# Preparing the last layer's first half batch in a lane of layer 2

## The chip, the cores and the metric

The kernel is one program for one core of a Trainium2 chip. The metric is device time of one execution in microseconds (us), lower is better; the figure quoted is the median of several runs. Everything is computed in fp32. Five engines run their own instruction streams in order and wait for each other through semaphores: TensorE (PE, matrix products), VectorE (DVE), ScalarE (ACT), GpSimd (POOL, which here issues the gathers and scatters) and SyncE (SP, which issues the other transfers).

## The reference

Four layers work on a residual `x` of 4 sequences, 1024 tokens each, 128 channels. Each layer adds half a feed-forward block, a whole "attention" block, and half the same feed-forward block again:

```python
x = x + 0.5 * L0_ffn(ln(x)); x = x + L0_attn(ln(x)); x = x + 0.5 * L0_ffn(ln(x))
x = x + 0.5 * L1_ffn(ln(x)); x = x + L1_attn(ln(x)); x = x + 0.5 * L1_ffn(ln(x))
x = x + 0.5 * L2_ffn(ln(x)); x = x + L2_attn(ln(x)); x = x + 0.5 * L2_ffn(ln(x))
x = x + 0.5 * L3_ffn(ln(x)); x = x + L3_attn(ln(x)); x = x + 0.5 * L3_ffn(ln(x))
```

`L2_ffn` is a mixture of 8 experts, of which each token uses the best 2 (128 -> 512 -> 128, relu). `L2_attn` is a linear attention with one decay `gamma`. Layer 3, cut to what matters:

```python
def L3_attn(x):                       # 16 heads of 8 channels, y_t depends on all t' < t
    xx = shift(x) - x                 # the token before, minus this one
    m = tanh((x + xx * maa_x) @ w1)   # five small mixes, one for each of w k v r g
    xw, xk, xv, xr, xg = (x + xx * (maa_i + m_i @ w2_i) for i in "wkvrg")
    r, k, v, g = xr @ W_r, xk @ W_k, xv @ W_v, silu(xg @ W_g)
    wdec = exp(-exp(time_decay + tanh(xw @ dw1) @ dw2))
    for t in range(T):                # the recurrence, for each head
        kv = outer(k[t], v[t]); y[t] = r[t] @ (S + u * kv); S = S * wdec[t] + kv
    return (groupnorm(y) * gamma + beta) * g @ W_o

def L3_ffn(x):                        # xr, xk mix a token with the one before
    return sigmoid(xr @ W_r.T) * (square(relu(xk @ W_k.T)) @ W_v.T)
```

## The kernel before, in words

The residual stays on the chip as four tiles `X[b]` (128 channels x 1024 tokens, `x0` to `x3`). `run` goes through the stages l0, l1_attn, l2 and l3; layer 1's feed-forward blocks are run inside l0 and l2.

**Lanes.** Within a stage, work is written as tasks: generators that record some instructions and then yield an estimated cost. `lanes` takes several lists of tasks. A task starts when the tasks that it names are done and the one ahead of it in its lane is finished; of the tasks that are running, the one with the lowest clock goes on. That settles the order in which the program is recorded. The framework below it then settles the order of each engine's stream, and adds the waits, also those for memory: a tile that is laid over the place of older tiles waits until these have been used for the last time. Pools are stacked from the left or the right end of the on-chip memory, and a pool that is opened later takes the place of one that was closed.

**Layer 2** (`layer2`, `macaron`). The tokens are routed and run through the experts in two groups, A = sequences 0 and 1, and Z = 2 and 3, and that twice (`n` = 0 ahead of the attention, 1 behind it). The lanes of the stage are: the four expert runs; the combines, which fetch the results of a sequence and add them to its `X`; two lanes with layer 1's last feed-forward blocks (`first0` to `first3`) and the attention of the four sequences (`middle0` to `middle3`); and the routes. `experts` works in blocks of 128 slots, 39 for a group: SP loads the block's expert weights (`e_w`, five buffers), POOL gathers 128 token rows (`e_xg`, L452), PE turns them (L456), multiplies up in four products and down in four (L229), ACT applies the bias and the relu between (`e_h`, L466), DVE adds the last bias (`e_y`, L477) and POOL scatters (`res`, L478). `combine` loads `c_y` from `res`, weighs (L508, L509), turns (L512) and adds. The last run of experts, n = 1 with group Z, starts when everything else of layer 2 but combine 10, 11 (sequences 0, 1) and combine 12, 13 is over.

`l2_decay` makes the decay matrix `G` and its row `grow` (L853 to L865) for the attention, in a pool of its own (`l2d`) at the right end. Nothing else needs them before `middle0`. They depend only on weights.

**Layer 3** (`layer3`). Eight units: four sequences, two halves of 512 tokens. Each unit has a front (`l3_ffn`, then `l3_prepare`, which makes `wdec`, `k`, `vals`, `r`, `g` and the first part of `y`), the recurrence (`l3_recur`), and an end (`l3_finish`, and `l3_ffn` again). There are five lanes: one of recurrences in the order 00, 10, 01, 11, 20, 30, 21, 31 (sequence, half), two of ends and two of fronts (even and odd sequences). The fronts of even sequences keep their tiles in `l3even` and those of odd ones in `l3odd`, at the right end. `normed` is the layer norm at the head of each part: centre (a product with `x`), square (`n_sq`), four small products, the root on ACT (`n_std`, L956), the reciprocal on DVE (`n_r`, L957), four products that spread it, and `xn` (L966). A whole stage ends before the next one starts to be recorded, so all eight fronts are recorded behind layer 2.

Of the kernel before, what the change touches and what calls it, by code (L numbers as in the profile page):

```python
# [18 lines left out]
B, S, D = 4, 1024, 128  # L19
# [188 lines left out]
class Macaron:  # L208
# [959 lines left out]
        v.tensor_tensor(X, X, o, ALU.add)  # L1168
        yield 6

    def layer3(self, f, t, c3):
        sb = lambda name, bufs=2, **k: self.tc.tile_pool(name=name, bufs=bufs, reuse_waits="tile", **k)
        with ExitStack() as ctx:
            enter = ctx.enter_context
            wave, accs, tail, prep = (
                enter(self.psum(name, n)) for name, n in (("l3wave", 2), ("l3acc", 1), ("l3tail", 2), ("l3prep", 3))
            )

            tmp, *front = (enter(sb(name, side="right")) for name in ("l3tmp", "l3even", "l3odd"))
            rec, *end = (enter(sb(name)) for name in ("l3rec", "l3ends0", "l3ends1"))  # L1180
            given, carries, seen = {}, {}, {}
            start = lambda f, *a: lambda: f(*a)
            units = [(b + i, h) for b in range(0, B, 2) for h in range(2) for i in range(2)]
            fronts, recs, ends = ([], []), [], ([], [])
            for b, h in units:
                u = f"{b}{h}"
                mine = given[b, h] = {}
                wp, wend = front[b % 2], end[b % 2]
                s = [seen.setdefault((b, i), {}) for i in range(3)]
                fronts[b % 2].extend([  # L1190
                    (f"ffn{u}0", (), start(self.l3_ffn, prep, tmp, wp, f, b, h, s[0])),
                    (f"prepare{u}", (), start(self.l3_prepare, prep, tmp, wp, t, c3, b, h, s[1], mine)),
                ])
                recs.append((f"recur{u}", (f"prepare{u}",), start(self.l3_recur, wave, accs, rec, c3, b, h, carries, mine)))
                ends[b % 2].extend([
                    (f"finish{u}", (f"recur{u}",), start(self.l3_finish, tail, wend, t, c3, b, h, mine)),
                    (f"ffn{u}1", (), start(self.l3_ffn, tail, tmp, wend, f, b, h, s[2])),
                ])
            self.lanes(recs, *ends, *fronts)
# [71 lines left out]
    def layer2(self, moe, m, right, enter, ffn):  # L1271
        A, Z = (0, 1), (2, 3)
        side, main = self.side, self.main
        decay = self.l2_decay(side, enter(right, "l2d"), m, self.c2)
        early = right.enter_context(ExitStack())
        pf = [enter(early, f"l1f1{i}") for i in range(2)]
        pa = []

        def swap():

            early.close()
            pa.extend(enter(right, f"l2a{i}") for i in range(2))
            yield 0

        def more(route):
# [12 lines left out]
        self.macaron("l2", moe, AF.Relu, ([A, Z], [A, Z]), marks, more)  # L1298

    def run(self, stages):  # L1300
        nc = self.nc
        self.X = []
# [14 lines left out]
        tags = {"l1a": "attn_w", "l3a": "attn_w", "c1": "attn_c", "c2": "attn_c", "c3": "attn_c"}  # L1317
        have = {}

        def weights(name):  # L1320
            if name not in have:
                have[name] = self.l1_weights() if name == "l1f" else self.load(name, tag=tags.get(name))
            return have[name]

        sb = lambda name, bufs=2, **k: self.tc.tile_pool(name=name, bufs=bufs, reuse_waits="tile", **k)
        for n, name in enumerate(stages):
            for s in stages[n : n + 2]:
                for w in needs[s]:
                    weights(w)
            if name in ("l0", "l2"):  # L1330
                with self.psum("main", 4) as self.main, self.psum("side", 4) as self.side, sb(name + "moe") as self.fp:
                    moe = dict(weights(name + "s"))
                    moe["both"] = self.t(self.res, [P, P + NE], "both", bufs=2)
                    nc.vector.tensor_copy(moe["both"][:, 0:P], self.c0["center"])
                    nc.scalar.copy(moe["both"][:, P:], self.centered(moe["rw"], NE))
                    with ExitStack() as right:
                        enter = lambda stack, name, bufs=2: stack.enter_context(sb(name, bufs, side="right"))
                        m = dict(weights(name + "a"))
                        ffn = lambda wp, ps, b: lambda: self.l1_ffn(ps, wp, weights("l1f"), b)
                        if name == "l2":  # L1340
                            self.c2 = weights("c2")
                        if name == "l0":
                            self.layer0(moe, m, right, enter, ffn)
                        else:
                            self.layer2(moe, m, right, enter, ffn)
            elif name == "l1_attn":
                with sb("ln1") as self.lnp:
                    self.l1_attn(weights("l1a"), weights("c1"))
            else:
                f, t, c3 = self.l3_ffn_weights(weights("l3f")), self.l3_time_weights(weights("l3a")), weights("c3")  # L1350
                self.layer3(f, t, c3)
        for b in range(B):
            nc.sync.dma_start(out=self.out[:, b * S : (b + 1) * S], in_=self.X[b])

# [35 lines left out]
```

## Time and profile before

| | us |
|---|---|
| median of 3 runs (3131.44 to 3135.03) | 3132.94 |
| the profiled execution, whole | 3239.76 |
| its span in the profile | 3237.5 |
| layer 1's attention ends (its last add to `x3`, L807) | 2030.6 |
| combine 11 ends, from here the last experts are alone | 2623.5 |
| last product of the last experts | 2722.0 |
| first product of layer 3 | 2742.6 |
| end of the span | 3237.5 |

The profile is of one execution, and it was longer than the runs without it. Its rows show, for a group of instructions, the engine, the operation, what it writes and reads, the shape, how many there were, how long they took, and the idle time ahead of them with what ended it. `x0`, `n_r` and the like are the program's tile names; L229 is the line of a helper through which nearly all products are recorded, so products are told apart by tile and shape. An fp32 product stands in the trace as two matmul records. PEclk is the clock that TensorE was granted in a stretch, 1.00 being full speed.

### The profile page before, as it was taken

To read this page: it belongs to the slowest core of one execution; us is meant where nothing else is said; L and a number is where in the kernel's file an instruction comes from. 1 tells how busy PE (TensorE), PEld (TensorE's weight loads), DVE (VectorE), ACT (ScalarE), POOL (GpSimd) and SP (SyncE) were. 2 spreads that over 40 slices of the span, in tenths; PEclk is the share of its full clock that TensorE was granted. 3 is DMA by queue.
4 is the path that set the end of the run, shared out by engine and by line. 5 is a ranking of instruction groups with operands and counts; after the bars stand their busy time and mean duration, and the time that the engine had idled before them with its cause. 6 is when DMAs were issued, how large, how long until landed. Compare 5 with 4: busy or idle time off the path is not lost. (4 is left out here: it accounts for less than half of the span.)

```text
span 3237.5 us, 47507 instructions
## 1 busy us (share of the span) xinstructions
PE 2766.3 (85%) x17694; PEld 1584.7 (49%) x17694; DVE 1834.3 (57%) x3214; ACT 1626.5 (50%) x3631; POOL 799.3 (25%) x748
## 2 busy tenths in 40 slices
PE   5877537778969999999999999987988976899997
PEld 4666415665633333333333333567877865334333
DVE  3476986774226676676677673452565622354764
ACT  3555524657712565566465666444453544345342
POOL 3566306552440000000000000046434463010110
PEclk8889758889977999999999999989998988788997
DMA  6656415563500000000000000057665675000000
GB/s 211 208 169 196 125 50 160 159 188 119 154 19 9 5 6 4 6 5 6 20 6 4 3 1 1 21 166 233 198 186 163 209 228 162 0 1 1 7 7 13
DMA packets 122886, 277.57 MB, mean 86 GB/s; under 512 B 18016, under 2 KB 67296, under 8 KB 122528
## 3 DMA queue, kind: packets, MB, share of 16 engines
q1 hardware_dynamic: 101792, 231.77, 23.7%
q0 software_dynamic: 20864, 42.77, 4.5%
q8 instruction: 140, 2.29, 0.3%
q14 instruction: 90, 0.74, 0.1%
HBM read 238.43 MB, written 31.85 MB: 83 GB/s over the span
## 5 line engine op out<-in xcount | busy, mean ns | idle before, releaser
L736 DVE TENSOR_REDUCE nm<-two 128x2 f32<-128x1024 f32 x512 | 626.6, 1224 | 290.8 <-PE s L229 271.4
L759 ACT ACTIVATE e<-s 128x512 f32<-128x512 f32 x1024 | 555.8, 595 | 408.7 <-PE s L229 405.7
L466 ACT ACTIVATE e_h<-bank,e_w 128x128 f32<-128x128 f32 x1304 | 451.0, 367 | 495.3 <-PE bank L229 382.9
L229 PE MATMUL bank<-e_x,e_w 128*128 128x128 f32 x2608 | 543.6, 312 | 127.9 <-ACT e_h L466 65.7
L229 PE MATMUL s<-qm,kz 32*128 32x512 f32 x2048 | 635.7, 645 | 0.8 <-ACT e L759 0.8
L229 PE MATMUL two<-kz,qz 32*128 32x512 f32 x2048 | 595.0, 666 | 21.4 <-POOL va L724 2.5
L452 POOL DMA_INDIRECT e_xg<-rows,g_source x326 | 331.6, 1017 | 822.1 <-DVE g_target L419 356.1
L229 PE MATMUL bank<-e_w,e_h 128*128 128x128 f32 x2608 | 475.5, 298 | 56.7 <-ACT e_h L466 31.3
L229 PEld LDWEIGHTS bank<-e_x,e_w 128*128 128x128 f32 x2608 | 413.4, 205 | 219.9 <-ACT e_h L466 113.1
L478 POOL DMA_INDIRECT res<-e_y,g_target x326 | 368.6, 1131 | 300.1 <-DVE e_y L477 135.4
L229 PEld LDWEIGHTS bank<-e_w,e_h 128*128 128x128 f32 x2608 | 387.6, 206 | 89.8 <-ACT e_h L466 46.6
L229 PE MATMUL o<-e,va 128*32 128x256 f32 x4096 | 329.2, 393 | 0.1
L229 PEld LDWEIGHTS two<-kz,qz 32*128 32x128 f32 x2048 | 160.1, 189 | 240.5 <-issue 163.3
L229 PEld LDWEIGHTS o<-e,va 128*32 128x32 f32 x4096 | 81.0, 108 | 391.8 <-issue 371.8
L458 DVE COPY e_x<-bank 128x128 f32<-128x128 f32 x326 | 92.7, 285 | 263.7 <-PE bank L456 139.7
L477 DVE TENSOR_TENSOR e_y<-bank,e_w 128x128 f32<-128x128 f32 x326 | 93.6, 287 | 213.9 <-PE bank L229 191.0
L229 PEld LDWEIGHTS s<-qm,kz 32*128 32x128 f32 x2048 | 207.0, 184 | 10.9 <-issue 7.8
L724 POOL COPY va<-vd 128x256 f32<-128x256 f32 x16 | 6.7, 431 | 626.2 <-PE o L229 537.9
L1131 POOL TENSOR_TENSOR z<-st,r 128x512 f32<-128x512 f32 x32 | 46.2, 1444 | 417.5 <-DVE st L1124 240.2
L456 PE MATMUL bank<-c,e_xg 128*128 128x128 f32 x326 | 97.0, 300 | 39.7 <-DMA e_xg<-rows,g_source 36.2
L466 ACT ACT_TABLE_LOAD x53 | 68.0, 1283 | 24.0 <-PE bank L229 18.0
L544 DVE TENSOR_TENSOR prod<-qkv 128x2048 f32<-128x2048 f32 x32 | 73.1, 2286 | 5.5 <-ACT qkv L536 5.5
(304 smaller groups left out, 3489.0 us busy)
## 6 DMA issues: line engine op xcount, KB each, us to landing
e_w<-in_l0m_dram SPq DMA_DIRECT2D x170, 578.0 KB
e_w<-in_l2m_dram SPq DMA_DIRECT2D x156, 578.0 KB
c_y<-res SPq DMA_DIRECT2D x32, 512.0 KB
rows<-g_xt SPq DMA_DIRECT2D x16, 512.0 KB
e_xg<-rows,g_source POOLq DMA_INDIRECT x326
res<-e_y,g_target POOLq DMA_INDIRECT x326
x<-in_x_dram SPq DMA_DIRECT2D x4, 512.0 KB
qz<-qd SPq DMA_DIRECT2D x64, 32.0 KB
```

The lines of the kernel that those rows point to most:

```text
L229: self.nc.tensor.matmul(out, lhsT, rhs, start=start, stop=stop)
L452: nc.gpsimd.indirect_dma_start(out=xg, out_offset=None, in_=rows[:, :], in_offset=at(source[:, k : k + 1]))
L456: nc.tensor.transpose(tp, xg, self.c0["ident"])
L458: nc.vector.tensor_copy(x, tp)
L466: nc.scalar.activation(h[:, fc, :], o[:, fc, :], func, bias=w[:, 2 * FC * P + fc : 2 * FC * P + fc + 1])
L477: nc.vector.tensor_tensor(y, o, w[:, MOE_W - D :], ALU.add)
L478: ins = nc.gpsimd.indirect_dma_start(out=res[:, :], out_offset=at(target[:, k : k + 1]), in_=y, in_offset=None)
L544: v.tensor_tensor(pr, q.unsqueeze(2).to_broadcast(sh), k.unsqueeze(1).to_broadcast(sh), ALU.mult)
L724: nc.gpsimd.tensor_copy(va[n % RING][:, :, :, 1 : 1 + HD], dense[b, "vd"][:, :, 32 * g4 : 32 * g4 + 32].rearrange("p t (h d) -> p t h d", ...
L736: v.tensor_reduce(nm[:, it, h, 2 * pair : 2 * pair + 2], s, AX.X, ALU.max, negate=True)
L759: nc.scalar.activation(es[g], s, AF.Exp, scale=scale)
L1131: (pool if i else v).tensor_tensor(z, st[:, 0:HALF], r, ALU.mult)
```

## The change

The front of layer 3's first unit (sequence 0, first half) becomes a lane of layer 2. A task `clear` waits until all four attentions of layer 2 are over, closes their pools, opens layer 3's pools `l3tmp` and `l3even` in their place, makes layer 3's scaled weights, and adds two tasks to its own lane: `ffn000`, which waits for combine 10, and `prepare00`. They use the `side` PSUM pool of layer 2. `layer3` then leaves this front out, and its first recurrence waits for nothing. So that the attention's pools can be closed ahead of layer 2's end, the pool `l2d` of the decay goes to the left end, where it lies in the place of layer 1's attention.

```diff
+    def l3_front(self, b, h, prep, wp, after=()):
+        l3, u = self.l3, f"{b}{h}"
+        f, t, c3 = l3["weights"]
+        mine = l3["given"].setdefault((b, h), {})
+        s = [l3["seen"].setdefault((b, i), {}) for i in range(2)]
+        return [
+            (f"ffn{u}0", after, lambda: self.l3_ffn(prep, l3["tmp"], wp, f, b, h, s[0])),
+            (f"prepare{u}", (), lambda: self.l3_prepare(prep, l3["tmp"], wp, t, c3, b, h, s[1], mine)),
+        ]
+
+    def l3_open(self):
+        sb = lambda name: self.l3_pools.enter_context(self.tc.tile_pool(name=name, bufs=2, reuse_waits="tile", side="right"))
+        w = self.weights
+        self.l3.update(
+            weights=(self.l3_ffn_weights(w("l3f")), self.l3_time_weights(w("l3a")), w("c3")),
+            given={}, seen={}, tmp=sb("l3tmp"), even=sb("l3even"), begun=[],
+        )
...
-            tmp, *front = (enter(sb(name, side="right")) for name in ("l3tmp", "l3even", "l3odd"))
+            tmp, given, seen = (l3[k] for k in ("tmp", "given", "seen"))
+            front = l3["even"], enter(sb("l3odd", side="right"))
...
-                fronts[b % 2].extend([
-                    (f"ffn{u}0", (), start(self.l3_ffn, prep, tmp, wp, f, b, h, s[0])),
-                    (f"prepare{u}", (), start(self.l3_prepare, prep, tmp, wp, t, c3, b, h, s[1], mine)),
-                ])
-                recs.append((f"recur{u}", (f"prepare{u}",), start(self.l3_recur, wave, accs, rec, c3, b, h, carries, mine)))
+                begun = (b, h) in l3["begun"]
+                if not begun:
+                    fronts[b % 2].extend(self.l3_front(b, h, prep, front[b % 2]))
+                mine = given[b, h]
+                s = {2: seen.setdefault((b, 2), {})}
+                after = () if begun else (f"prepare{u}",)
+                recs.append((f"recur{u}", after, start(self.l3_recur, wave, accs, rec, c3, b, h, carries, mine)))
...
     def lanes(self, *lanes):
-        lanes = [list(lane) for lane in lanes]
...
-        decay = self.l2_decay(side, enter(right, "l2d"), m, self.c2)
+        decay = self.l2_decay(side, enter(right, "l2d", side="left"), m, self.c2)
+        late = right.enter_context(ExitStack())
...
-            pa.extend(enter(right, f"l2a{i}") for i in range(2))
+            pa.extend(enter(late, f"l2a{i}") for i in range(2))
             yield 0
+
+        def clear():
+            late.close()
+            self.l3_open()
+            self.l3["begun"].append((0, 0))
+            lane.extend(self.l3_front(0, 0, side, self.l3["even"], ("combine10",)))
+            yield 0
+
+        lane = [("clear", [f"middle{b}" for b in range(B)], clear)] if self.goes_on else []
...
                     route(1, A, "middle0", "middle1", "combine01"), route(1, Z, "middle2", "middle3", "combine03"),
                 ],
+                lane,
```

The order of the instructions on each engine, as the two programs have it: the front's products stand between those of about 12.5 expert blocks, beginning at the end of combine 11, and 24 blocks follow them. Layer 3's first recurrence stands right behind combine 13 on DVE. The 23 instructions of `l2_decay` that stood in two places among layer 1's attention on DVE stand behind the last add to `x3` (L807), ahead of layer 2's first `xc` (L614), and PE multiplies `G` ahead of the first product with `x0`. On SP the load of layer 3's constants `c3`, which takes the place of the decay's, goes behind the load of `l3a`; the other orders of SP and POOL differ only by exchanges of neighbours.

More of the change, by code (lines that the diff above doesn't have):

```diff
@@ L1169, in l3_finish, with layer3 @@
         yield 6
-    def layer3(self, f, t, c3):
+    def l3_front(self, b, h, prep, wp, after=()):
[14 more added lines that the diff above has]
+        )
+    def layer3(self):
+        if not self.l3:
+            self.l3_open()
+        l3 = self.l3
+        f, t, c3 = l3["weights"]
         sb = lambda name, bufs=2, **k: self.tc.tile_pool(name=name, bufs=bufs, reuse_waits="tile", **k)
@@ L1177, in layer3 @@
             )
-            tmp, *front = (enter(sb(name, side="right")) for name in ("l3tmp", "l3even", "l3odd"))
+            tmp, given, seen = (l3[k] for k in ("tmp", "given", "seen"))
+            front = l3["even"], enter(sb("l3odd", side="right"))
             rec, *end = (enter(sb(name)) for name in ("l3rec", "l3ends0", "l3ends1"))
-            given, carries, seen = {}, {}, {}
+            carries = {}
             start = lambda f, *a: lambda: f(*a)
@@ L1186, in layer3 @@
                 u = f"{b}{h}"
-                mine = given[b, h] = {}
-                wp, wend = front[b % 2], end[b % 2]
-                s = [seen.setdefault((b, i), {}) for i in range(3)]
-                fronts[b % 2].extend([
-                    (f"ffn{u}0", (), start(self.l3_ffn, prep, tmp, wp, f, b, h, s[0])),
-                    (f"prepare{u}", (), start(self.l3_prepare, prep, tmp, wp, t, c3, b, h, s[1], mine)),
-                ])
-                recs.append((f"recur{u}", (f"prepare{u}",), start(self.l3_recur, wave, accs, rec, c3, b, h, carries, mine)))
+                wend = end[b % 2]
+                begun = (b, h) in l3["begun"]
[5 more added lines that the diff above has]
+                recs.append((f"recur{u}", after, start(self.l3_recur, wave, accs, rec, c3, b, h, carries, mine)))
                 ends[b % 2].extend([
@@ L1281, in swap @@
             early.close()
-            pa.extend(enter(right, f"l2a{i}") for i in range(2))
+            pa.extend(enter(late, f"l2a{i}") for i in range(2))
             yield 0
+        def clear():
+            late.close()
+            self.l3_open()
+            self.l3["begun"].append((0, 0))
+            lane.extend(self.l3_front(0, 0, side, self.l3["even"], ("combine10",)))
+            yield 0
+        lane = [("clear", [f"middle{b}" for b in range(B)], clear)] if self.goes_on else []
         def more(route):
@@ L1301, in run @@
         nc = self.nc
-        self.X = []
+        self.X, self.l3, self.l3_pools, self.goes_on = [], {}, ExitStack(), "l3" in stages
         self.c0 = self.load("c0")
@@ L1323, in weights @@
             return have[name]
+        self.weights = weights
         sb = lambda name, bufs=2, **k: self.tc.tile_pool(name=name, bufs=bufs, reuse_waits="tile", **k)
@@ L1336, in run @@
                     with ExitStack() as right:
-                        enter = lambda stack, name, bufs=2: stack.enter_context(sb(name, bufs, side="right"))
+                        enter = lambda stack, name, bufs=2, side="right": stack.enter_context(sb(name, bufs, side=side))
                         m = dict(weights(name + "a"))
@@ L1349, in run @@
             else:
-                f, t, c3 = self.l3_ffn_weights(weights("l3f")), self.l3_time_weights(weights("l3a")), weights("c3")
-                self.layer3(f, t, c3)
+                self.layer3()
+                self.l3_pools.close()
         for b in range(B):
```

## The prediction

> **What bounds the kernel now.** I read the page's slices first, then the change's three places: a table of windows, the timeline of PE, the groups of one window. The page has PE busy 85% of the span; what counts is which wait ends last in each place. Columns of the first fence: stretch, length, then busy us of PE, PE's weight loads, DVE, ACT, POOL, then PE's granted clock and the DMA.
>
> ```profile
> 2450.00:2550.00 100.00, 98.19 (x698) 88.21 (x698) 63.46 (x205) 41.50 (x110) 46.54 (x48) 0.99 0.55 169
> 2623.00:2722.00 99.00, 81.91 (x581) 70.08 (x579) 17.95 (x67) 46.08 (x136) 58.85 (x61) 1.00 0.74 226
> 2722.00:2742.00 20.00, 4.97 (x17) 3.03 (x17) 6.25 (x20) 4.89 (x16) 0.97 (x1) 0.60 0.41 112
> 2742.00:2813.00 71.00, 61.27 (x157) 27.56 (x157) 16.39 (x37) 28.04 (x44) 0.00 (x0) 0.75 0.00 0
> 2813.00:2853.00 40.00, 38.41 (x98) 17.23 (x102) 22.95 (x42) 15.98 (x30) 6.02 (x4) 0.79 0.00 1
> 2853.00:3158.00 305.00, 291.44 (x911) 121.41 (x904) 182.47 (x276) 137.21 (x246) 34.72 (x24) 0.91 0.01 4
> 3158.00:3237.00 79.00, 58.78 (x168) 26.07 (x166) 31.87 (x44) 20.93 (x38) 5.48 (x5) 0.78 0.03 14
> ```
>
> The last experts alone (2623 to 2722) leave PE 18% idle: no engine is full, and their 33.9 blocks (305 products, nine a block) take 2.92 us each. Beside the attention (2450 to 2550) PE is full. Layer 3's middle, 2853 to 3158, is PE's: 291 of 305 us. Its head is PE's too, at clock 0.75. The next fences show PE at that seam: the drain of the experts, 9.00 and 5.58 us of waiting for the last combines, then the first two fronts; and its clock.
>
> ```profile
> 2722.04 0.49 PE L229 MATMUL bank<-e_w,e_h 128*128 128x128 f32 x2 [0.23 <-ACT e_h L466]
> 2731.53 2.01 PE L512 MATMUL bank<-c,c_y 128*128 128x128 f32 x7 [9.00 <-DVE c_y L509]
> ...
> 2761.65 1.02 PE L229 MATMUL bank<-xn,now_k 128*128 128x512 f32 x2
> 2762.51 1.02 PE L229 MATMUL bank<-xn,past_k 128*128 128x512 f32 x2
> ...
> 2776.22 3.89 PE L229 MATMUL bank<-t,attn_w 128*128 128x512 f32 x4 [2.39 <-DVE t L1042]
> ```
>
> ```profile
> 2748.00:2754.00 6.00, 5.31 (x18) 0.50 0.00 0
> 2754.00:2760.00 6.00, 5.35 (x13) 0.50 0.00 0
> 2760.00:2766.00 6.00, 6.00 (x16) 1.00 0.00 0
> ```
>
> **What a front costs.** At full clock a 512-wide product starts every 0.86 us (2761.65, 2762.51). `ffn000`: 6 such (5.2), and its norm's four 1-wide and four 128-wide products (8 records in about 0.5 and 0.95): 6.6 us. `prepare000`: 16 such (13.8), two side-by-side pairs of 1.06, a norm of 1.5: 17.4. Together 24.0 us of PE at full clock. With the recurrence (6.4), the finish (4.1) and the second `ffn` (6.6) a unit is 41.1, layer 3 eight times that, 329.
>
> **Layer 3 loses a front.** Counted in the program's order, 211 us of those 329 lie between the rows at 2853 and 3158, where the first and sixth recurrences' sums end; they take 305 us, 1.445 us for each full-clock us (clock 0.91, changes of weights and shapes, short waits). 24.0 x 1.445 = 34.7 us. It is off the end's path only as far as PE stays the bound. At the head the first recurrence now runs beside the next two `ffn`: eight kv (0.68), eight scans (1.21) and four z (0.67) are 18 us of DVE, which had only 16.4 us of work in the head's 71, so it fits, but the fronts' norms queue behind the scans: I give back 2 us. **-33**, from -42 (idle PE in the head filled as well) to -22 (the head's chains stretch, and only the head's 24 us at full clock are won).
>
> **The head's clock.** The trace has PE at 0.50 from about 2725 to 2760, though it was busy 5.3 of 6 us from 2748. The Trainium skill (TensorE: Matmul & The Clock Gate, Part 1) has half clock only until about 3.4 us of sustained activity. By that rule the cold stretch ends near 2746 and only some 3 us of layer 3's first work is slow; by the trace it is 17 us. Does moving the front out of a cold stretch gain more? By the trace no: the gap of 2722 to 2742 stays, and the same cold stretch then falls on the next front. So I count full-clock us at the middle's rate. By the rule the head would cost some 7 us less before and after alike, and the sum would be the same.
>
> **The last experts gain a front.** 24.0 us of PE come among 12.5 blocks that took 36.5 us. What is free? In 2450 to 2550, PE full, 24 blocks went beside 44.5 us of attention products (same spacings, 0.11 a record and in proportion to width), so a packed block costs (100 - 44.5) / 24 = 2.3 us. Then 12.5 x 2.3 + 24.0 = 52.8, **+16.3**. To that come waits of the front's own chain, since PE takes its products in order and the blocks behind them wait:
>
> ```profile
> L229 PE MATMUL bank<-c,n_r 128*128 128x128 f32 x32 | 8.3, 440 | 3.4 <-DVE n_r L957 3.4
> L229 PE MATMUL bank<-c,n_sq 128*128 128x1 f32 x32 | 6.0, 310 | 2.7 <-ACT n_sq L950 2.7
> L229 PE MATMUL bank<-t,attn_w 128*128 128x512 f32 x4 | 3.1, 860 | 2.4 <-DVE t L1042 2.4
> ```
>
> These rows of the head (2745 to 2813), with 0.7 ahead of `x`, are 9.2 us for two fronts, 4.6 for one; the blocks between fill about half: +2.5. ACT gets eleven times about 0.6 and five table loads of 1.28, 13 to 16 us, where it is 46% busy; a relu caught behind a load makes PE wait for `e_h`: +2. Against it, while PE is held the weights of the next blocks land, and one or two blocks then run at 2.3 or 2.56 (the drain's pace) instead of 2.92 us until these are used up: -4. Sum **+17**, from +7 (idle PE takes nearly all, catch-up of two more blocks) to +30 (none is used). The loads and gathers are not more; they are only later, since SP's `e_w` waits for a buffer that the delayed `e_y` frees, and POOL's gathers for PE's turns.
>
> **The decay moves.** Layer 2's decay leaves layer 1's attention. There it did cost something:
>
> ```profile
> 1581.93 0.23 DVE L857 COPY G<-attn_c 128x128 f32<-128x128 f32 x1 [1.99 <-DMA attn_c<-in_c_dram]
> ...
> 1586.01 1.21 DVE L736 TENSOR_REDUCE nm<-two 128x2 f32<-128x1024 f32 x1
> ```
>
> The reduce at 1586.01 stood behind the series though its product began at 1582.6, and PE idled 1.94 us for it: **-2**. At the new place DVE has 8 x 0.16, 15 x about 0.26, then two copies of 0.6 and a reciprocal between: 7 us behind the last L807, so `G` is done near 2037, and the first product with `x0`, at 2026.2 before, waits on PE until then. `x0`'s norm takes 6 us more: both first products come at 2043 instead of 2037.4 and 2040.5. Six gate and up products were done by 2045.0 and will be near 2048.5: **+4**, to +8 if PE comes back cold, +1 if the order of `x1` covers it. It is not hidden: PE is full from 2045, and routes and experts wait for these. The load of `c3`, now behind the decay, has until layer 3; on SP the row writes behind it come 50 us later.
>
> **Sum.** -33 + 17 - 2 + 4 = -14 us in the profiled execution of 3239.76. The median is 3132.94, 3.3% less; I scale to -13.5 and predict **3120**. The measurement can tell about 0.2%, 6.3 us.
>
> **Rivals.**
> 1. *The blocks pay for it all (slower).* Every link of the front's chain holds PE, because few block products stand between: behind the first norm's small products there are three, 0.6 us, against a table load, a root and a reciprocal of 1.28 + 0.26 + 0.17. Then 24 us, 4.6 us of links and 6.4 us of table loads all add, with 5 us more for blocks that miss their turn: +40, and -33 + 40 + 2 = +9, 3142. It decides from +31, when the 12.5 blocks take 5.4 us each. For it: PE's order is fixed. Against: the attention's chains packed well. 0.24.
> 2. *The experts hide it (much faster).* The weights set the pace, so front and blocks only fill PE's 18%, and the loads run ahead: +7, sum -24, 3109. For it: DMA 0.74 busy at 226 GB/s, blocks of 1.9 us at 2624.66 to 2628.45. Against: five buffers, of which four are in use. 0.18.
> 3. *Layer 3 is not shortened by its products.* The recurrences are one lane, and if their turns with DVE and POOL set the middle, a missing front only leaves PE idle: layer 3 gains 12, the sum is +7, 3140. Against: PE 291 of 305. 0.12. That the front is not moved at all is excluded by the order.
>
> The likeliest, 0.46, gives 3120 with 3111 to 3130. Faster by over 0.2%: 0.39 of it, rival 2 whole: 0.57. Slower: 0.20 of rival 1, 0.05 of rival 3, 0.01 of the likeliest: 0.26. The rest, 0.17, within. Range 3104 to 3145: the lower half of rival 2 and the upper third of rival 1 are cut.
>
> **What would show it.** The profile after should have the experts from combine 11 to their last product at about 116 us instead of 99, PE over 90% busy in the front's stretch; the first recurrence's sum about 35 us behind layer 3's first product (110 before), layer 3 some 33 us shorter; PE's products with `x0` in layer 2 about 10 us after L807. Wrong if the experts grow by over 30 us (rival 1), under 10 (rival 2), or layer 3 shortens by under 20 (rival 3).

## The result, and the profile after

The changed kernel takes 3118.43 us (median of 22 runs, 3108.86 to 3130.17); before takes 3129.45 us on the same chip (22 runs, 3123.61 to 3135.53). The ratio is 0.9966, with an interval of 0.9957 to 0.9976: 10.6 us less by the ratio, 7.5 to 13.5 by the interval. The prediction was 3120, from 13.5 us less. The experiments ran on three chips on which before took 3251 to 3266 us; what that makes of the change is part of the explanation. The record does not name the chip of this first comparison. The profiled execution of the changed kernel has a span of 3118.9 us.

First the table of windows of the changed kernel: stretch, length, busy us of PE, PE's weight loads, DVE, ACT and POOL, PE's granted clock, DMA share, GB/s.

```profile
2540.00:2591.00 51.00, 49.94 (x256) 32.31 (x255) 14.39 (x36) 28.78 (x66) 19.77 (x20) 1.00 0.52 154
2591.00:2645.00 54.00, 53.71 (x416) 50.42 (x414) 14.01 (x48) 32.69 (x98) 39.48 (x41) 1.00 0.87 279
2645.00:2665.00 20.00, 6.06 (x21) 3.27 (x21) 6.28 (x20) 4.88 (x16) 1.52 (x2) 0.57 0.41 111
2665.00:2736.00 71.00, 67.64 (x193) 29.76 (x193) 33.83 (x67) 28.07 (x52) 5.65 (x4) 0.81 0.00 1
2736.00:2776.00 40.00, 39.22 (x109) 18.86 (x109) 17.68 (x32) 16.86 (x29) 3.10 (x2) 0.83 0.00 1
2776.00:3040.00 264.00, 256.15 (x770) 105.64 (x769) 153.24 (x233) 112.22 (x204) 28.95 (x20) 0.89 0.01 4
3040.00:3118.00 78.00, 59.70 (x173) 27.59 (x172) 37.28 (x51) 22.48 (x42) 8.41 (x6) 0.76 0.03 14
```

The first row is the front among the expert blocks: PE is busy 49.9 of 51 us. In the second, the 24.4 blocks behind it, PE has hardly any idle time: 2.22 us a block, at 279 GB/s, where before's profile had 2.91 us and 226 GB/s. The third row is the drain, as empty as before. In layer 3's head (fourth row) PE is busy 67.6 of 71 us, against 61.3; DVE has twice the work, since the first recurrence now runs there.

The seam in PE's timeline (start, length, engine, line, operation; in brackets the idle time and what ended it), and behind it PE's clock (stretch, length, PE busy, clock, DMA share, GB/s):

```profile
2644.94 0.49 PE L229 MATMUL bank<-e_w,e_h 128*128 128x128 f32 x2 [0.23 <-ACT e_h L466]
2645.36 1.13 PE L1026 MATMUL wave<-vals,attn_c 32*128 32x512 f32 x4
2654.34 2.05 PE L512 MATMUL bank<-c,c_y 128*128 128x128 f32 x7 [7.86 <-DVE c_y L509]
...
2662.89 2.05 PE L512 MATMUL bank<-c,c_y 128*128 128x128 f32 x7 [5.64 <-DVE c_y L509]
```

```profile
2665.00:2671.00 6.00, 5.67 (x13) 0.50 0.01 3
2671.00:2677.00 6.00, 5.22 (x10) 0.50 0.00 0
2677.00:2683.00 6.00, 6.00 (x16) 0.50 0.00 1
2683.00:2689.00 6.00, 6.00 (x23) 0.52 0.00 0
2689.00:2695.00 6.00, 6.00 (x16) 1.00 0.00 0
```

The recurrence's first products (`wave`) run at the start of the drain; the next ones come only behind it, at 2667.44. The cold stretch is not gone; it lasts some 24 us into layer 3. Of the front's own waits the groups of the front's stretch show almost nothing:

```profile
L229 PE MATMUL bank<-c,n_r 128*128 128x128 f32 x16 | 2.2, 280 | 0.6 <-DVE n_r L957 0.6
L229 PE MATMUL bank<-c,n_sq 128*128 128x1 f32 x16 | 2.1, 253 | 0.0
L229 PE MATMUL bank<-t,attn_w 128*128 128x512 f32 x2 | 1.0, 594 | 0.0
```

0.6 us, where the head of before had 8.5 us in these rows for two fronts: the blocks between fill it.

### The profile page after: what moved, and what is told of

It is laid out like the page before. It is cut to its first block, busy times and chain, and to the rows that moved or that the text cites. A ratio compares the mean times of both kernels' runs of the same rounds, so it can differ in the third digit from the quotient of the medians.

```text
span 3118.9 us, 47516 instructions
## 1 busy us (share of the span) xinstructions
PE 2740.2 (88%) x17694; PEld 1580.9 (51%) x17694; DVE 1831.6 (59%) x3214; ACT 1616.8 (52%) x3627; POOL 796.0 (26%) x748
## 4 chain that ended last, share of the span: by engine, by line
PE 67%; DVE 6%; ACT 3%; DMA 3%; POOL 2%; issue 1%; POOLq 0%; SPq 0%; ACTq 0%; DVEq 0%
PE bank L229 32%; PE two L229 18%; PE o L229 8%; PE s L229 5%; DVE nm L736 2%; PE wave L1026 2%; DMA c_y<-res 1%; DMA e_xg<-rows,g_source 1%; ACT e_h L466 1%; PE bank L1026 1%; PE bank L456 1%; PE acc L1026 1%; POOL kz L669 0%; DMA e_w<-in_l2m_dram 0%; DMA res<-e_y,g_target 0%
## 5 line engine op out<-in xcount | busy, mean ns | idle before, releaser
L736 DVE TENSOR_REDUCE nm<-two 128x2 f32<-128x1024 f32 x512 | 626.0, 1224 | 289.8 <-PE s L229 269.6
L229 PE MATMUL bank<-e_w,e_h 128*128 128x128 f32 x2608 | 465.6, 293 | 26.3 <-ACT e_h L466 17.4
L229 PEld LDWEIGHTS bank<-e_w,e_h 128*128 128x128 f32 x2608 | 381.6, 203 | 49.7 <-ACT e_h L466 30.5
L458 DVE COPY e_x<-bank 128x128 f32<-128x128 f32 x326 | 92.7, 285 | 199.4 <-PE bank L456 181.1
L1131 POOL TENSOR_TENSOR z<-st,r 128x512 f32<-128x512 f32 x32 | 46.1, 1441 | 384.8 <-DVE st L1124 318.6
L1026 PE MATMUL wave<-vals,attn_c 32*128 32x512 f32 x128 | 74.3, 761 | 3.7 <-DVE kv L1117 3.6
```

The costliest lines, as they stand in the source:

```text
L229: self.nc.tensor.matmul(out, lhsT, rhs, start=start, stop=stop)
L458: nc.vector.tensor_copy(x, tp)
L736: v.tensor_reduce(nm[:, it, h, 2 * pair : 2 * pair + 2], s, AX.X, ALU.max, negate=True)
L1026: i = self.nc.tensor.matmul(out, lhsT, rhs, start=start, stop=stop).ins
L1131: (pool if i else v).tensor_tensor(z, st[:, 0:HALF], r, ALU.mult)
```

## Where the time went, in all profiles

All profiles, cut at the same events: the first and last row of layer 1's attention (L736, L807), the last product of combine 03 and of combine 11, the last expert product, the last product of combine 13, the end. us of each piece. The kernels are those of the experiments below; rows with one number in the first column ran on one chip (a dash: not known).

| chip | kernel | to the attention | attention | to combine 03 | to combine 11 | last experts | drain | layer 3 |
|---|---|---|---|---|---|---|---|---|
| - | before (first profile) | 968.3 | 1062.3 | 414.4 | 178.5 | 99.0 | 19.8 | 495.2 |
| - | after | 924.2 | 1057.6 | 393.4 | 164.9 | 105.3 | 19.9 | 453.6 |
| 5 | ctrl (before) | 984.6 | 1062.3 | 417.8 | 182.0 | 104.2 | 20.1 | 493.2 |
| 5 | decay_left | 986.5 | 1056.8 | 433.6 | 181.5 | 104.1 | 20.1 | 492.3 |
| 5 | front_only | 984.0 | 1059.8 | 416.0 | 176.8 | 120.8 | 20.1 | 449.5 |
| 5 | late76 | 987.5 | 1056.6 | 434.1 | 180.6 | 113.9 | 26.0 | 455.0 |
| 8 | ctrl2 (before) | 978.2 | 1062.6 | 414.0 | 177.6 | 102.7 | 19.8 | 495.9 |
| 8 | after2 | 989.8 | 1057.7 | 422.1 | 179.4 | 121.3 | 19.8 | 440.9 |
| 8 | late76_right | 979.5 | 1059.7 | 415.4 | 177.8 | 109.1 | 25.7 | 445.3 |
| 8 | front_plus | 972.8 | 1059.8 | 411.6 | 177.3 | 121.6 | 19.4 | 472.9 |
| 1 | ctrl3 (before) | 981.7 | 1060.5 | 421.7 | 182.0 | 105.3 | 19.8 | 495.7 |
| 1 | warm_before | 978.5 | 1062.3 | 418.9 | 177.9 | 107.1 | 19.3 | 493.9 |
| 1 | warm_front | 977.6 | 1062.3 | 418.6 | 177.1 | 121.3 | 19.6 | 450.2 |
| 1 | ffn_only | 972.0 | 1061.4 | 421.5 | 182.3 | 107.9 | 19.9 | 457.4 |

Two things are read from it. All four profiles of before are of one kind, with spans of 3237.5 to 3266.8 us, also the one that the prediction had; none is of an execution of 3130. And after and after2 are the same kernel, 112 us apart: the attention is equal to 0.1 us, and after2 is longer in every stretch with experts (the first, the third, the fourth and the fifth column, 125 us together); its layer 3 was 13 us shorter. Executions like that of after are called short below, and those like after2 and the four of before long.

It is easy to take the weights for the cause, since the long executions move fewer GB/s, but the traces speak against it. In after2, for the blocks behind the front (2700 to 2770), these are all the waits of PE, and the largest of SP's, which issues the weights (us in total, times, the longest):

```profile
PE bank L229 <- ACT e_h L466: 8.0, 9, 2.0
PE bank L229 <- issue: 1.6, 5, 0.6
PE bank L229 <- DVE e_x L458: 0.4, 1, 0.4
```

```profile
SPq L450 <- DVE e_y L477: 21.2, 10, 4.2
```

PE waits for no load; the loads wait for buffers that the blocks free. Followed one by one from issue to last packet to first product, the weights of after2 were in place 1.4 us or more ahead of their use (4.5 in the median), those of before 2.6 or more, those of ctrl2 3.7 or more. In after, the short execution, it was 1.7 us in the median, and once nothing. So late weights are not the cause, and the low rate goes with the slow blocks without making them slow. What does differ is when the results of PE arrive: DVE copies a turned block (`e_x`, L458) at most 0.14 us behind the end of PE's record in after, up to 1.6 us behind it in after2 and 1.9 in before. What holds them back no run shows, so the cause of the long executions stays open.

## The experiments

Ratios are against before on the same chip, with their 95% intervals.

**Before once more** (`ctrl`, no edit).

> The kernel before, profiled once more. The first profile of before was about 107 us longer than its median, and had its last experts at 2.92 us a block; after has them at 2.16 us a block behind the front, PE full. Theory (that execution's transfers were slow): here the span is near 3127, the stretch from combine 11's end to the last expert product is about 77 us (2.25 us a block, PE over 93% busy), the tail 20 us, layer 3 about 494 us. Rival (the front itself lets the weights run ahead): the stretch is again near 99 us, 2.9 us a block, and the 107 us are elsewhere.

It took 3266.4 us, its last experts 104.2 us. The theory needed a 3130 us execution to show itself, and this was none, so the two were not told apart by the time. Slow transfers as its reason do not fit the trace: here too the weights landed 2.7 us or more ahead of their first product. ctrl2 and ctrl3 below repeat the run, with the same outcome.

**The decay alone** (`decay_left`): before, with

```diff
-        decay = self.l2_decay(side, enter(right, "l2d"), m, self.c2)
+        decay = self.l2_decay(side, enter(right, "l2d", side="left"), m, self.c2)
...
-                        enter = lambda stack, name, bufs=2: stack.enter_context(sb(name, bufs, side="right"))
+                        enter = lambda stack, name, bufs=2, side="right": stack.enter_context(sb(name, bufs, side=side))
```

> Before, with only the decay's pool moved to the left end, so that its DVE instructions go behind the last L807. Theory of the prediction: +2 us against before (-2 in the attention at its old place, +4 at the first products with x0). Rival 1: PE comes back cold and x0 is late: +6 to +8. Rival 2: the order with x1 first covers it: -2 to 0.

Ratio 1.002 (1.0006 to 1.0033), 6.5 us slower: rival 1. The table has 4 to 6 us less in the attention, where -2 was expected, and 16 us more before combine 03 (12 to 20 against the several profiles of before; after2 has 0 to 8 more). The timeline of decay_left, all engines, and then that of ctrl2, which has the decay at its old place:

```profile
2042.55 0.75 DVE L807 SCALAR_TENSOR_TENSOR x<-two,attn_w,x 128x512 f32<-128x512 f32 x1 [3.50 <-PE two L229]
2043.22 0.14 DVE L853 COPY gp<-l2a 128x1 f32<-128x1 f32 x1
...
2048.32 0.29 DVE L861 TENSOR_TENSOR G<-G,Gf 128x128 f32<-128x128 f32 x1
...
2049.90 3.78 PE L229 MATMUL bank<-x,c 128*128 128x512 f32 x4
...
2058.21 3.21 PE L229 MATMUL bank<-xn,l1f_wg 128*128 128x512 f32 x4
```

```profile
2040.13 0.74 DVE L807 SCALAR_TENSOR_TENSOR x<-two,attn_w,x 128x512 f32<-128x512 f32 x1
2041.39 1.96 PE L229 MATMUL bank<-x,c 128*128 128x512 f32 x4
2047.17 1.02 PE L229 MATMUL bank<-xn,l1f_wg 128*128 128x512 f32 x2
```

And PE's clock in decay_left (length, PE busy, clock, DMA, GB/s):

```profile
2044.00:2048.00 4.00, 2.72 (x19) 0.90 0.55 161
2048.00:2052.00 4.00, 3.55 (x7) 0.50 0.28 76
```

The first gate product comes 14.9 us after L807's end instead of 6.3. PE stood idle behind the series on DVE, its clock went to 0.50, and the four products with `x` took 3.78 us instead of 1.96. So the place is right, and the size was +8.6, at the bound of +8 that the prediction had named for a cold PE. What decay_left (and late76) lost beyond this before combine 03 is not settled.

**The front alone** (`front_only`): after, with the decay's pool at the right end, below layer 3's pools.

```diff
-        decay = self.l2_decay(side, enter(right, "l2d", side="left"), m, self.c2)
+        decay = self.l2_decay(side, enter(self.l3_pools, "l2d"), m, self.c2)
```

> After, with the decay's pool kept at the right end, below layer 3's pools, so that the decay is made where before makes it; only the front is moved. Theory: the decay's move costs 2 us, so this gains 12 to 13 us against before where after gained 10.6. If the decay's move costs 6 to 8: 17 to 19 us gained. If it gains: 9 us or less.

Ratio 0.9907 (0.9882 to 0.9933), 30 us less. None of the three numbers fits, because they were reckoned from the 10.6 us of the first comparison, and on this chip the change is worth more.

**The change again** (`after2`, no edit) and before beside it (`ctrl2`).

> The kernel before, profiled again. Before ran at 3129 beside after, but at 3266 beside the first experiments, and both profiles of it so far (3237.5 and 3264.2) show the slow transfers: last experts 99 and 104 us for the same products. If before runs near 3130 here: theory, these 34 blocks have their weights in time and PE sets their pace, about 78 us for the stretch (105.3 in after, less 24 to 27 for the front). If it runs near 3266: about 104 us again. Rival: the stretch is 99 to 104 us whatever the time of the whole.

> The changed kernel again. Theory: its gain depends on how long the weights take. If before is near 3266 here, its blocks alone leave PE idle, the last experts grow by 16 to 17 us as with the front alone, layer 3 loses 42, the decay costs 6: 20 to 24 us less than before (ratio 0.993). If before is near 3130, the last experts grow by 26, the sum is -10 (0.9966, as at first). Rival: the gain is the same 10 us on both, and the 30 us of the front alone were the decay's doing.

Before ran at 3251 here, so ctrl2 again told nothing of a 3130 us execution. after2 has a ratio of 0.9925 (0.9903 to 0.9948), 24.5 us less: the theory's number, though not for its reason, since the weights were in place in time. It is 6 us worse than the front alone, which is what decay_left measured for the decay (the two intervals overlap). Its windows for the front and for the blocks behind it (same columns as the first fence), and then ctrl2's for the last experts and for layer 3's head:

```profile
2649.00:2700.00 51.00, 49.94 (x256) 32.32 (x254) 14.34 (x35) 28.81 (x66) 18.85 (x19) 1.00 0.46 145
2700.00:2770.00 70.00, 59.74 (x417) 53.35 (x414) 13.61 (x48) 33.21 (x98) 39.77 (x41) 0.95 0.68 213
```

```profile
2632.00:2735.00 103.00, 84.61 (x582) 73.68 (x581) 18.15 (x67) 46.58 (x136) 59.00 (x61) 0.96 0.68 218
...
2755.00:2826.00 71.00, 61.47 (x157) 27.50 (x157) 16.08 (x34) 27.82 (x43) 0.00 (x0) 0.75 0.00 0
```

The front's stretch is PE's and takes 51 us on both chips, to the hundredth of PE's busy time. What lies around it differs: the 24.4 blocks behind it take 54.2 us in after and 70.2 in after2, 2.22 and 2.88 us each. The 10.1 blocks inside (the order of the program had suggested 12.5) would have taken 30.5 us alone at ctrl2's 3.02 us, so the front costs 20.6 there, less 3.4 us of catch-up behind it: 17, and 18.6 by the whole stretch. At 2.22 us a block, before's 34.0 blocks would take 75.5 us, and after's 105.3 are 30 more. That 30 is an estimate, since no profile of a short execution of before was to be had. After's blocks keep their pace to the end, with the weights landing a steady 1.4 to 2.2 us ahead of use for the loads of 2604 to 2627, so it is no passing effect of loads that ran ahead behind the front. The estimate fits the sum of the first comparison: about -41 in layer 3, -5 and +8 for the decay, +30 make -8, and -10.6 was measured.

**The front held back** (`late76`, and `late76_right` with the decay as in front_only).

```diff
-            lane.extend(self.l3_front(0, 0, side, self.l3["even"], ("combine10",)))
+            lane.append(("wait", ("combine10",), lambda: iter([76])))
+            lane.extend(self.l3_front(0, 0, side, self.l3["even"]))
```

> After, with the front held back in its lane, so that it starts some 21 blocks later: about 14 us of its products at full clock stand behind the last expert product, among the products of combines 12 and 13, where PE waited 14 us. Theory (PE is full in the last experts, so the front costs there what its products cost, and only idle PE is free): these 14 us become free, 10 to 14 us less than after, 21 to 25 less than before. Rival (the experts hide most of the front, or the front's chain in the tail holds up the combines' products and layer 3): no better than after, -10 to 0 against before.

> The front alone, the decay where before has it, and the front held back so that about 14 us of its products stand behind the last expert product. From late76 (0.9904 with the decay on the left, which cost 0.2%): if before is near 3266, 0.988 to 0.989, 5 to 8 us better than the front alone (0.9907). If before is near 3130, where PE is full beside the last experts, the tail's idle time counts fully: 8 to 12 us better than the front alone, 0.990 to 0.992. Rival (the front's chain in the tail holds the combines' products back, as their products at 2790 against 9 us behind the last expert product suggest): no better than the front alone.

0.9904 (0.9876 to 0.9932) and 0.9913 (0.9895 to 0.993): no better than the front alone, the rival's side. Late76, with the decay moved, is not behind late76_right, so the 6 us of the decay do not show in this pair, whose intervals overlap; its profile is of the longest of its six runs, 22 us above their median. In late76_right the last experts shrink to 109.1 us, but the drain grows from 20 to 25.7. Its PE timeline there:

```profile
2741.34 2.00 PE L229 MATMUL bank<-t,attn_w 128*128 128x512 f32 x4
...
2750.38 1.50 PE L229 MATMUL bank<-t,attn_w 64*128 64x512 f32 x2 [1.87 <-ACT t L1079]
2751.82 2.08 PE L1026 MATMUL bank<-t,attn_w 32*128 32x512 f32 x4
2753.82 3.78 PE L229 MATMUL bank<-xn,attn_w 128*128 128x512 f32 x4
...
2759.33 1.04 PE L512 MATMUL bank<-c,c_y 128*128 128x128 f32 x8
```

With no blocks between, a tanh on ACT holds PE 1.87 us, the clock halves, the pair of products at 2753.82 takes twice its time, and the combine's products, ready about 9 us behind the last expert product, start 18 us behind it.

**More of layer 3 moved** (`front_plus`): front_only, and the feed-forward half of the next front of sequence 0.

```diff
+            lane.append(self.l3_front(0, 1, side, self.l3["even"])[0])
...
-                    fronts[b % 2].extend(self.l3_front(b, h, prep, front[b % 2]))
+                    fronts[b % 2].extend(self.l3_front(b, h, prep, front[b % 2])[(b, h) == (0, 1) :])
```

> The front alone, the decay where before has it, and one more part of layer 3 brought over: the first half of the next front (the feed-forward of sequence 0, second half, 6.6 us of PE at full clock) behind it in the same lane. Theory: layer 3 is PE's and loses in proportion to products, 6.6 x 1.45 to 1.75 = 10 to 12 us more; the last experts grow by 4.5 (weights late) to 7 (PE full): 3 to 7 us better than the front alone. Rival (layer 3's gain of 42 came from the first recurrence starting at once, not from the products): layer 3 gains 0 to 3 more, and the whole is 2 to 6 us worse than the front alone.

Ratio 0.9975 (0.9958 to 0.9993), 22 us worse than the front alone by the ratios, and against both sides of the expectation in size: the last experts took no more (121.6), but layer 3, with 6.6 us less to do, took 23 us **more** than in front_only. One of its 16 runs took 3217.9 us, at a mean clock of 0.909 where the others have 0.893 to 0.900, so the loss is not in every execution.

**Less moved** (`ffn_only`): front_only with `ffn000` alone in the lane, `prepare000` in layer 3.

```diff
-            self.l3["begun"].append((0, 0))
-            lane.extend(self.l3_front(0, 0, side, self.l3["even"], ("combine10",)))
+            lane.append(self.l3_front(0, 0, side, self.l3["even"], ("combine10",))[0])
...
-                    fronts[b % 2].extend(self.l3_front(b, h, prep, front[b % 2]))
+                    fronts[b % 2].extend(self.l3_front(b, h, prep, front[b % 2])[(b, h) == (0, 0) :])
```

> Only the first half of the front (ffn000, 6.6 of its 24.0 us of PE) is moved, the decay where before has it, prepare000 recorded in layer 3. Theory of the prediction (layer 3 shortens in proportion to the products taken out): layer 3 -12, last experts +5, 7 us less than before (0.998). Rival (what counts is that the first recurrence can start at once, and that PE is not left waiting in the head): layer 3 -5 or less, the whole 0 to -2 us (0.9995 to 1.000).

Ratio 0.9897 (0.987 to 0.9925), 33.6 us less: neither. A quarter of the front's products brings layer 3 from 495.7 to 457.4, most of what the whole front brings, and costs the experts 2.6 us instead of 16 to 19 (among themselves the profiles of before differ by 6 there). The adds that end a recurrence, of ctrl2, ffn_only, front_only and front_plus in this order (times of the first and the last of the eight):

```profile
L1137 DVE TENSOR_TENSOR y<-y,acc x8: 686/688/689, 2867.0 to 3207.1; 128x512 f32<-128x512 f32 x8
```

```profile
L1137 DVE TENSOR_TENSOR y<-y,acc x8: 677/687/689, 2839.7 to 3182.4; 128x512 f32<-128x512 f32 x8
```

```profile
L1137 DVE TENSOR_TENSOR y<-y,acc x8: 657/687/689, 2818.6 to 3186.3; 128x512 f32<-128x512 f32 x8
```

```profile
L1137 DVE TENSOR_TENSOR y<-y,acc x8: 681/687/689, 2799.6 to 3194.4; 128x512 f32<-128x512 f32 x8
```

Counted from the last product of combine 13 (2755.0, 2764.9, 2777.4, 2762.6), the first is at 112, 75, 41 and 37 us, and the last at 452, 418, 409 and 432. The first recurrence gets earlier from each to the next. The last does not follow.

**PE kept busy in the drain** (`warm_before`, `warm_front`): before, and front_only, with idle products of a constant ahead of the products of combines 12 and 13, their results unused (62 and 25 products in warm_before, 38 and 25 in warm_front).

```diff
+WARM = 62, 25
...
+        if plan.get("warm"):
+            filler = self.t(ps, [P, HALF], "bank")
+            for _ in range(WARM[n]):
+                self.mm(filler[:, 0:P], self.c0["center"], self.c0["center"])
         for h in range(2):
             tp = self.t(ps, [P, 4, P], "bank")
...
-            return plans.setdefault((n, group), {"mark": marks[n, group]})
+            return plans.setdefault((n, group), {"mark": marks[n, group], "warm": (name, n, group) == ("l2", 1, (2, 3))})
```

> The kernel before, profiled a fourth time, to lie beside the three runs of this group. If before is near 3130 here: last experts about 78 us instead of 99 to 104 (PE sets their pace). If it is near 3260: layer 3 at 493 to 496 us, last experts 99 to 104, as before. Rival: a time near 3130 with 99 to 104 us for the last experts.

> Before, with idle products of a constant (128x128, results unused) put on PE where it waits for combines 12 and 13: about 41 and 25 of them, 9.0 and 5.5 us. Theory (PE's idle time there is what halves its clock in layer 3's head, where before shows 0.65 to 0.74 over the first 50 us): the first 50 us go at 0.8 or more, layer 3 is 6 to 10 us shorter, ratio 0.997 to 0.998. Rival (the head waits for its chains, PE idle 10 us in the first 50): a faster clock only leaves PE more idle, layer 3 0 to 3 us shorter, ratio 0.999 to 1.001.

> The front alone, the decay where before has it, with the same idle products (about 36 and 25) in the waits for combines 12 and 13. Front alone had half clock from 15 us ahead of layer 3 to 15.6 us into it. Theory: those 15.6 us at half speed cost about 7; layer 3 goes from 445 to 450 to about 440, ratio 0.988 to 0.989 (front alone 0.9907). Rival (the half clock comes from something other than the idle tail, or chains bound the head): layer 3 unchanged, ratio 0.990 to 0.992.

Before ran at 3263 here; ctrl3 is a control for layer 3 alone (495.7). warm_before has 1.0002 (0.9985 to 1.0019), layer 3 at 493.9; warm_front 0.9913 (0.9886 to 0.9941), layer 3 at 450.2: the rival both times. The windows of warm_before (length, PE busy, clock, DMA, GB/s) and the waits behind them (lines of this kernel are 2 or 6 higher):

```profile
2744.00:2764.00 20.00, 19.24 (x154) 1.00 0.41 113
...
2764.00:2766.00 2.00, 1.31 (x5) 1.00 0.00 0
2766.00:2768.00 2.00, 1.03 (x8) 0.66 0.00 0
2768.00:2770.00 2.00, 1.78 (x8) 0.50 0.00 0
```

```profile
2763.99 0.33 PE L518 MATMUL bank<-c,c_y 128*128 128x128 f32 x1 [0.53 <-DVE c_y L515]
...
2765.86 1.17 PE L231 MATMUL bank<-c,n_sq 128*128 128x1 f32 x8 [0.69 <-ACT n_sq L956]
2768.22 2.05 PE L231 MATMUL bank<-c,n_r 128*128 128x128 f32 x8 [1.19 <-DVE n_r L963]
```

PE went through the drain at full clock and lost it between 2766 and 2768, some 2.5 us into layer 3, behind waits of 0.53 us for the last combine and 0.69 us inside its own norm; the 1.19 us came when it was halved already. The long idle time of the drain is not needed to make the head cold.

## What layer 3 is made of

The table splits layer 3's length: PE idle; PE busy, each moment counted with its granted clock (what the work would take at full clock); and the rest, what busy PE lost to half clock. Worked out from PE's records and the granted clock of each trace.

| kernel | length | idle | work at full clock | lost to half clock |
|---|---|---|---|---|
| ctrl2 (before) | 495.9 | 45.5 | 387.4 | 63.0 |
| after | 453.6 | 30.9 | 357.4 | 65.3 |
| after2 | 440.9 | 29.6 | 358.2 | 53.1 |
| front_only | 449.5 | 30.5 | 357.6 | 61.3 |
| ffn_only | 457.4 | 31.6 | 378.2 | 47.7 |
| front_plus | 472.9 | 44.7 | 347.7 | 80.5 |

The whole front takes 30 us of work and 15 us of waiting out. `ffn000` alone takes 9 us of work out, and the same 14 us of waiting, and 15 us of half clock. front_plus takes 40 us of work out, but the waiting is back and half clock costs 18 us more than in before. Work comes out in proportion to the products; the rest of what moves (a third for the whole front, three quarters for `ffn000`) follows from how the lanes mesh. Each row is one execution, and even for one kernel the loss to half clock differs by 12 us (after and after2), so in that column only larger differences count.

In before, layer 3 opens with two `ffn` chains and nothing to put between their steps, so PE waits 9.5 us in the first 71 and its clock stays low. With `ffn000` done it opens with steps of different kinds (4.7 us of waiting), with the whole front done also with a recurrence (3.0 to 3.8). In front_plus the second recurrence to be had early is 01, but the lane takes 10 and 11 around it, and PE waits 8.5 us between 100 and 150 us of layer 3 (5.4 of them for `z` on POOL, L1131), where front_only waits 0.8: the extra work went to a unit whose turn had not come. This is read from the traces; no run took the order of the lanes alone apart.

## Why the prediction was right, and where it was not

The number and the sign held; the sum held partly by errors that cancel. By its steps:

- **The last experts, +17.** Right for the executions that the profile was of: 120.8 to 121.3 against 102.7 to 105.3 on the same chips, +16 to +19, with the front's stretch at 51 us, PE full, and the blocks behind it quicker by 0.14 us each, as said. But the weights, by which the prediction explained this catch-up, were in place ahead of their use in before too. The 0.6 us of the front's own waits show that +2.5 for them was too much. The step that failed was to carry this sum over to the median by its ratio of 0.967. The 107 us between profile and median are no uniform stretch: the attention is the same to 0.1 us on both kinds, and the difference sits in the expert stretches. In the short executions, as after's profile has them, PE has no idle time there for the front to use (busy 53.71 of 54 us), and the front costs about 30 by the estimate above. The prediction had the ratio before it and should have asked where the 107 us lay.
- **Layer 3 loses a front, -33.** Measured -38 to -55 for the whole front against before on the same chip, mostly beyond the range's end of -42. The term "24.0 x 1.445" mixed three things that don't scale alike: 24.0 us of products are 30 us of work, and the rate's other part, waits and half clock, went its own way. The "2 us" given back for the head's chains had the wrong sign: the head's waiting fell by 6, layer 3's by 15. ffn_only shows the failed assumption plainest: -38 by 27% of the products.
- **The head's clock.** The row (0.50 until 2760 though busy from 2748) was rightly preferred to the rule in the Trainium skill (TensorE: Matmul & The Clock Gate, Part 1), but both readings took the drain for the cause of the cold stretch. warm_before has no idle drain and the same layer 3. The page's section "Why this matters for your kernels" wants no idle gaps over about 3 us between bursts of products; here gaps of 0.53 and 0.69 us within 3 us were followed by half clock, so keeping to that rule is not enough. Nor are gaps the whole of it, as the last section shows.
- **The decay moves, -2 and +4.** Measured -4 to -6 and +8 or more, while decay_left as a whole is +6.5 by the ratio; PE came back cold, which the text had as its upper bound.
- **Sum.** On the chips of the experiments the steps are now about -46, +18 and +6.5, -21, and 24.5 was measured (17 to 32). On the first chip about +30 stands in place of +18, and 10.6 was measured. That the number came so near is luck: on the first chip layer 3 gave 42 for 33 and the experts cost about 30 for 17, and these errors cancel. The forecast of 13.5 lies between the two measurements, and its mechanism, a saved stretch of layer 3 paid back in part by the last experts, is the one that the traces show.
- **Rivals.** Rival 1 was nearly right on its main term (the experts near +30 in short executions) but not from chains, which cost 0.6 us, and layer 3 gave more than it allowed. Rival 2, the experts hiding the front, is out: the front's stretch is PE's on both chips, and it is not the weights that set the blocks' pace in the long executions. Rival 3, layer 3 not following its products, was wrong as priced but right as a warning, as front_plus and ffn_only show.

No version stands clear above the others: ffn_only (0.9897), front_only (0.9907) and late76_right (0.9913) overlap, all of them with the decay at its old place, and so does late76 (0.9904) with the decay moved; after2 (0.9925) is 6 us behind, with an interval that overlaps theirs. ffn_only leaves the last experts nearly alone, so it should keep more of its gain in short executions; that was not run.

## What to carry to other kernels

If a profile is some per cent longer than the median, find the stretches in which it is longer before scaling a sum: a cost that is hidden in the long execution may be bare in the short one. Before naming late weights as the reason, follow some loads from issue to landing to first use: a low transfer rate can be the outcome of the wait and not its cause. A stage with PE busy 90% of the time is not priced by its products alone: split it into work at full clock, waits and half clock, and expect the last two to follow the order of the work. To break up a head of parallel chains that all wait at once, moving the first short link out can be worth nearly as much as moving the whole of it.

## What the runs showed of the hardware

- The same program took 3118.9 us in one profile and 3230.9 in another. The stretches with experts are 125 us longer in the second, layer 3 is 13 us shorter. Behind the front it is 2.22 and 2.88 us a block for the same 24.4 blocks, at 279 and 213 GB/s, though the weights had landed by their first product in both.
- PE's clock went to half behind waits of only 0.53 and 0.69 us in warm_before, and stayed there for 13.6 us (2766.7 to 2780.3). That the waits did it is not shown. In after it also halved behind 8 us in which PE's records leave no gap (stretch, length, PE busy, clock, DMA share, GB/s):

```profile
2745.60:2753.60 8.00, 8.00 (x30) 1.00 0.01 2
2753.60:2760.40 6.80, 6.80 (x15) 0.50 0.00 1
```

- In warm_before PE was kept at work by idle products until layer 3 began, and did not carry its clock far into it (1.00 until 2766, 0.50 from 2768).
